# Two table changes of the activation engine put on even slots, with the C product behind the slot's second scan

## The chip, the cores and the metric

The kernel runs on one core of one Trainium2 chip. The metric is device time in microseconds (us). The core's engines run side by side, each working through its own queue in order: PE multiplies matrices into PSUM, DVE works elementwise and does the scans, ACT evaluates functions, POOL does elementwise work on SBUF, and SP issues most of the DMAs.

## The reference, cut to what matters

Two layers are applied to an input of 4 images, 512 channels and 64x64 positions. The first is a state-space layer (Mamba), run on the 512 channels in four chunks of 128, the second a linear attention. The change touches the first layer. Cut down, for one chunk of one image:

```python
xi, z = jnp.split(jnp.einsum('bld,ed->ble', x, in_proj_w), 2, axis=-1)
xc  = silu(causal_conv4(xi) + conv_b)                  # 256 inner channels
dbc = jnp.einsum('bld,ed->ble', xc, x_proj_w)          # dt (8 columns), B (16), C (16)
dt  = softplus(einsum(dbc[..., :8], dt_proj_w) + dt_proj_b)
# for every token t, 256 channels x 16 states:
h = exp(dt_t[:, :, None] * A) * h + (dt_t * x_t)[:, :, None] * B_t[:, None, :]
y = jnp.einsum('bds,bs->bd', h, C_t)
# then
out = einsum((y + xc * D) * silu(z), out_proj_w) + skip * x
```

A layer norm stands ahead of the chunks and another behind them, followed by a 512x512 projection that is added to the input. The attention layer then needs statistics of the whole image before it can start.

## The kernel before, in words

**Steps and slots.** The tokens of an image (4096) are cut into 8 tiles of 512 (`T`). A step `n` is one chunk `c` (0 to 3) of one tile of one image: 4 images x 8 tiles x 4 chunks = 128 steps (line 1006). A step has 16 slots `s` (`SLOTS`, line 674). The 256 channels x 16 states of a step are laid out as 32 blocks of 128 partitions x 512 tokens: two channel halves `e`, four groups of states `q` and four blocks `j`. A slot handles two blocks, so two slots (an even one with `jj == 0`, an odd one with `jj == 1`) share one h tile of four blocks. There are two h tiles in turn (line 733).

**A slot** (`slot`, line 725). POOL builds the input of the slot two ahead, `bx = d * B` (`drive`, line 721). DVE does two scans (line 739); each reads a decay `dA` from PSUM, which ACT has made with an exponential (`decay`, line 713) three scans ahead (`LEAD`, three PSUM buffers: the decay for scan k+3 is issued behind scan k, whose buffer it takes). In the even slot, after its first scan, DVE multiplies the previous pair's h tile by C (`product`, line 759), for 384 of the 512 columns; POOL does the other 128 in the odd slot before (line 751). Then `fold_states` (line 761) has PE make the next C in PSUM (`c_row`, one buffer, so it waits for the product), and sum h over the states into `y` by eight matmul records (the fold); where a channel half begins (the products in slots 2 and 10), the D term's diagonal matmuls go ahead of the fold. The next pair but one may write its h tile only when the fold is done.

**What else a slot carries** (`after`, line 1108, called at the slot's end). Everything else of the step is dealt out by hand over the slots, and stands in each engine's queue behind the slot's scans:

| slot | before the change |
|---|---|
| 1 | half 1 of the step's dt and dt*x is spread over partitions (SP, line 639); gate of the previous step (POOL, line 781) |
| 2 | `time_banks`: matmuls of dt for the next step into two PSUM banks `pt` (PE) |
| 3 | softplus table loaded, `time_steps` (two softplus, line 620), exponential table loaded again (ACT) |
| 3, 5, 6, 7 | four half convolutions of step n+2 (`front`, four matmul records each, PE); 8, 9: the z half |
| 4 | `to_rows`: `dt*x` (POOL, line 628), whose two writes `d_rows` to DRAM follow one slot later (SP, line 631); `out_proj` of the previous step (PE, 12 records) |
| 6 | `with_skip` copies out_proj's result (ACT, line 792) |
| 9 | gate of the current step; half 0 of the next step is spread |
| 10 | silu of step n+2 between two table loads (ACT, line 1048) |
| 12 to 15 | x projection of step n+2 |

**Filler.** The layer norms and projections (`ahead`, `late`) and the attention of the previous image (`rest`) are generators that are asked for one piece at a time, at the end of a slot (lines 1161 to 1171). They share three PSUM banks `ps_w` with the rest: a piece that needs a bank must find fewer than `limit` held, which is 1 in slots 1 to 5 and 2 otherwise. PE's time is planned by a credit: each slot adds 3.5 matmul units (one unit is an fp32 matmul of 512 columns) less what the slot's own work took, capped at 2.6; a piece of the queues `late` and `rest` begins only while the credit is positive, and one that has begun (`"more"`) is finished in the next slot. Vector operations over a whole tile (2.26 us) are marked `"wide"` and wait for a slot in `AWAY`, in which ACT is away for its table change.

`AWAY` therefore names the slots of the two table changes. The lines that decide are these:

```python
    AWAY = (3, 10)
...
            if i == 0 and jj == 0 and g:
                product(g - 1)
                fold_states(g - 1, last)
...
                    limit[0] = 1 if 0 < s < 6 else 2
                    credit = min(credit + 3.5 - (work["mm"] - seen), 2.6)
```

Of the kernel before, what the change touches and what calls it, by code (L numbers as in the profile page):

```python
# [24 lines left out]
def kernel(  # L25
# [90 lines left out]
    limit, norming = [0], []  # L116
# [258 lines left out]
    def bc(v, n):  # L375
        return v.unsqueeze(1).to_broadcast([P, n, v.shape[-1]])
# [295 lines left out]

    JJ = NJ // 2
    SLOTS = NH * NQ * JJ
    AWAY = (3, 10)

    def place(g):

        n, r = divmod(g, SLOTS)
        e, r = divmod(r, NQ * JJ)  # L680
        return n, e, *divmod(r, JJ)
# [10 lines left out]
    def b_row(g):  # L692
        n, e, q, _ = place(g)
        b_all[g // JJ] = wk.tile([P, T], F32, tag="b_all", name=f"b_all_{g}", bufs=3)
        for_states(b_all[g // JJ], fs[n]["b_rows"], q)

    def c_tail(g):
        n, e, q, _ = place(g)
        c_sb[g // JJ] = wk.tile([P, T - CUT], F32, tag="c_sb", name=f"c_sb_{g}", bufs=2)
        for_states(c_sb[g // JJ], fs[n]["c_rows"], q)  # L700
# [7 lines left out]
    def decay(k):  # L708

        n, e, q, jj = place(k // 2)  # L710
        j = jj * 2 + k % 2
        dAs[k] = ps_d.tile([P, T], F32, tag="dA", name=f"dA_{k}")
        nc.scalar.activation(  # L713
            dAs[k], fs[n]["d_all", e][:, 0, j, :], AF.Exp, scale=a_t[:, e, j, q : q + 1]
        )

    def drive(g):

        n, e, q, jj = place(g)
        bxs[g] = wk.tile([P, 2, T], F32, tag="bx", name=f"bx_{g}", bufs=3)  # L720
        nc.gpsimd.tensor_tensor(  # L721
            bxs[g], fs[n]["d_all", e][:, 1, jj * 2 : jj * 2 + 2, :], bc(b_all[g // JJ], 2), ALU.mult
        )

    def slot(g, last, after):
        n, e, q, jj = place(g)
        b, t, c = steps[n]
        if g + 2 < last:
            drive(g + 2)
        if jj == 0:  # L730
            if g + 3 * JJ < last:
                b_row(g + 3 * JJ)
            hs[g // JJ] = wk.tile([P, NJ, T], F32, tag="h", name=f"h_{g}", bufs=2)
        elif g + 1 < last:
            c_tail(g + 1)
        h = hs[g // JJ]
        for i in range(2):
            j = jj * 2 + i
            nc.vector.tensor_tensor_scan(  # L739
                h[:, j, :], dAs.pop(2 * g + i), bxs[g][:, i, :],  # L740
                0.0 if t == 0 else st[:, c, e, q, j : j + 1], ALU.mult, ALU.add,
            )
            if 2 * g + i + LEAD < 2 * last:
                decay(2 * g + i + LEAD)
            if i == 0 and jj == 0 and g:
                product(g - 1)
                fold_states(g - 1, last)
        del bxs[g]
        if jj == JJ - 1:
            nc.gpsimd.tensor_copy(st[:, c, e, q, :], h[:, :, T - 1])  # L750
            nc.gpsimd.tensor_tensor(  # L751
                h[:, :, CUT:], h[:, :, CUT:], bc(c_sb.pop(g // JJ), NJ), ALU.mult
            )
        after()

    def product(g):

        own = hs[g // JJ][:, :, :CUT]
        nc.vector.tensor_tensor(own, own, bc(c_all.pop(g // JJ), NJ), ALU.mult)  # L759
# [283 lines left out]
    def step_inputs(n):  # L1043
        b, t, c = steps[n]
        return inputs(fs[n], xn[b, t], c, names[n])
# [6 lines left out]
    def add_to(queue, pieces):  # L1052
        queue.append([pieces, None])
# [40 lines left out]
    with tc.manual_schedule():  # L1094
        credit, seen, mix, held[0], held_x[0] = 0.0, work["mm"], iter(()), 0, 0
        for n, (b, t, c) in enumerate(steps):
            f, nm = fs[n], names[n]
            before = fs[n - 1] if n else None
            nxt = fs[n + 1] if n + 1 < N else None
            front = step_inputs(n + 2) if n + 2 < N else iter(())  # L1100
            last_mix, mix = mix, mixers(fs[n + 2], names[n + 2]) if n + 2 < N else iter(())
            if c == 0 and (t + 1 < NT or b + 1 < B):
                add_to(ahead, tile_norm(b, t + 1) if t + 1 < NT else tile_norm(b + 1, 0))
            if c == 0 and t == 0 and b + 1 < B:
                add_to(light, input_norm(b + 1))
            assert c != 2 or not ahead
            for s in range(SLOTS):
                def after():
                    nonlocal credit, seen
                    now[0] = n * SLOTS + s  # L1110
                    for what in [w for at, w in due if at <= now[0]]:
                        what()
                    due[:] = [d for d in due if d[0] > now[0]]
                    if s == 0 and before is not None:
                        take_y(before, n - 1, 1)
                    if s == SLOTS // 2:
                        take_y(f, n, 0)
                    if s < 2:
                        next(last_mix, None)
                    if s == 1:  # L1120
                        spread(f, 1, nm)
                        if before is not None:
                            gate(before, 1)
                    if s == 2 and nxt is not None:
                        time_banks(nxt, names[n + 1])
                    if s == 3 and nxt is not None:
                        nc.scalar.preload_act_table_set("softplus")
                        time_steps(nxt, names[n + 1])
                        nc.scalar.preload_act_table_set("natural_log_exp_and_others")
                    if s == 6 and before is not None:  # L1130
                        pb_, pt_, pc_ = steps[n - 1]
                        with_skip(before, xn[pb_, pt_], pc_)
                        if pc_ == NC - 1:
                            add_to(late, leave(pb_, pt_))
                    if s in (3, 5, 6, 7, 8, 9):
                        next(front, None)
                    if s == 4 and nxt is not None:
                        to_rows(nxt, 0, names[n + 1])
                        to_rows(nxt, 1, names[n + 1])
                    if s == 4 and before is not None:  # L1140
                        pb_, pt_, pc_ = steps[n - 1]
                        out_proj(before, xn[pb_, pt_], pc_, names[n - 1])
                    if s == 9:
                        gate(f, 0)
                        if nxt is not None:
                            spread(nxt, 0, names[n + 1])
                    if s == 10 and n + 2 < N:
                        silu(n + 2)
                        nc.scalar.preload_act_table_set("natural_log_exp_and_others")
                    if s >= 12:  # L1150
                        next(mix, None)
                    may = [
                        what for k, what in ((0, "wide"), (1, "one ahead"), (2, "two ahead"))
                        if any(a - 2 * k <= s <= a - k for a in AWAY) or (k == 2 and s == SLOTS - 1)
                    ]
                    if light and light[0][1] == "wait" or s in AWAY and not any(
                        q and q[0][1] == "wide" for q in (ahead, late)
                    ):
                        one(light)

                    limit[0] = 1 if 0 < s < 6 else 2
                    credit = min(credit + 3.5 - (work["mm"] - seen), 2.6)
                    busy = False
                    for queue in (ahead, late, rest):
                        kind = queue[0][1] if queue else None
                        if queue is ahead or kind == "free" or credit > 0 or kind == "more" and not busy:
                            start = work["mm"]
                            one(queue, ANYWHERE if queue is ahead and (c, s) > (1, 4) else may)
                            credit -= work["mm"] - start
                            busy = busy or work["mm"] - start > 1  # L1170
                    seen = work["mm"]

                slot(n * SLOTS + s, N * SLOTS, after)
            fs[n - 1].clear() if n else None
        product(N * SLOTS - 1)
        fold_states(N * SLOTS - 1, N * SLOTS)
        now[0] = None
        for _, what in due:
            what()
# [60 lines left out]
```

## Time and profile before

| | |
|---|---|
| median of three runs | 7947.08 us (7937.27 to 7951.86) |
| the profiled execution | 7963.09 us |
| its span, first to last instruction | 7961.4 us |
| mean granted TensorE clock | 0.897 |
| first scan starts, last scan ends | 122.4 us, 7493.4 us |
| busy: DVE, POOL, PE, ACT | 6977.7, 6880.5, 6453.6, 5507.6 us |
| one scan, one C product (DVE) | 1264, 1726 ns |
| one bx, one tail product (POOL) | 2367, 1270 ns |
| one decay, one table load (ACT) | 687, 1283 ns |
| silu of a step; one softplus (ACT) | 1911, 684 ns |
| dt*x of a step (POOL) | 2361 ns |

In a group's line, the text ahead of the bar is line, engine, operation, what it writes and reads with shapes, and the count. Behind the bar stand busy time in us, mean time of one in ns, then the engine's idle time just before the group and what ended most of it. A line of the timeline has start and duration in us, then the instruction; `x4` says that four alike are merged, and the bracket gives the idle time before the first and what ended it. Where several semaphores were waited for, the one named is the last by the profile, and need not be the real cause.

### The profile page before, as it was taken

How to read it: one execution, taken by the hardware profiler on the slowest of the kernel's cores; microseconds unless marked ns; L12 is line 12 of the kernel's file. 1: busy time of each engine (PE TensorE's matmuls, PEld its weight loads, DVE VectorE, ACT ScalarE, POOL GpSimd, SP SyncE). 2: the span in 40 equal slices, each digit the busy share in tenths (PEclk: the TensorE clock that was granted, in tenths of full speed). 3: DMA queues.
4: the chain of work that ended last, by engine and by line, in shares of the span. 5: the costliest groups of instructions: out<-in, count | busy, mean ns of one | idle time of the engine just before them, and what ended most of it. 6: DMA issues, size and time to landing. Idle time of an engine off the chain costs nothing.

```text
span 7961.4 us, 90563 instructions
## 1 busy us (share of the span) xinstructions
PE 6453.6 (81%) x24835; PEld 2120.0 (27%) x24880; DVE 6977.7 (88%) x5766; ACT 5507.6 (69%) x8321; POOL 6880.5 (86%) x4597
## 2 busy tenths in 40 slices
PE   5676777677789888888788888898688888888599
PEld 1121212112223222322222223332122332322144
DVE  5999999999999999989999999998999999988600
ACT  4667777777777777767777777677777777777421
POOL 4999999999999899989999899898999999889600
PEclk7888888888899999998899999899899999999799
DMA  5666666666666666777766666677666666676402
GB/s 154 167 168 166 151 155 159 160 155 167 169 179 162 151 163 159 174 189 175 174 155 171 171 157 161 155 185 189 156 167 163 161 161 159 145 194 180 112 32 90
DMA packets 829184, 1265.87 MB, mean 159 GB/s; under 512 B 183912, under 2 KB 317560, under 8 KB 816384
## 3 DMA queue, kind: packets, MB, share of 16 engines
q1 hardware_dynamic: 804736, 1222.32, 61.1%
q0 software_dynamic: 16896, 33.56, 2.4%
q10 hardware_dynamic: 7040, 4.20, 0.2%
q8 instruction: 195, 3.19, 0.2%
q14 instruction: 317, 2.60, 0.1%
HBM read 1052.78 MB, written 206.57 MB: 158 GB/s over the span
## 4 chain that ended last, share of the span: by engine, by line
DVE 33%; PE 21%; ACT 15%; DMA 12%; issue 8%; SPq 6%; POOL 6%; POOLq 0%; ACTq 0%; DVEq 0%
DVE h L739 22%; DVE h L759 9%; DMA d_all<-d_rows 7%; ACT dA L713 5%; PE pq L124 5%; POOL bx L721 4%; PE pc L124 4%; SPq L688 3%; PE y L124 3%; PE pr L124 3%; SPq L639 2%; DMA c_sb<-c_rows 2%; ACT xz L1048 2%; PE po L124 2%; ACT L1048 1%
## 5 line engine op out<-in xcount | busy, mean ns | idle before, releaser
L721 POOL TENSOR_TENSOR bx<-d_all,b_all 128x1024 f32<-128x1024 f32 x2048 | 4824.7, 2367 | 213.3 <-DVE h L739 195.1
L739 DVE TENSOR_TENSOR_SCAN h<-dA,st,bx 128x512 f32<-128x512 f32 x3584 | 4358.9, 1264 | 358.7 <-ACT dA L713 159.0
L713 ACT ACTIVATE dA<-d_all,a_t 128x512 f32<-128x512 f32 x4096 | 2752.9, 687 | 1568.5 <-DVE h L739 1521.8
L759 DVE TENSOR_TENSOR h<-h,c_all 128x1536 f32<-128x1536 f32 x1024 | 1767.5, 1726 | 0.1
L751 POOL TENSOR_TENSOR h<-h,c_sb 128x512 f32<-128x512 f32 x1024 | 1300.2, 1270 | 190.2 <-DMA c_sb<-c_rows 95.2
L124 PE MATMUL y<-h,fold 128*32 128x512 f32 x8192 | 1271.2, 696 | 71.6 <-POOL h L751 67.4
L124 PE MATMUL c_all<-parts,sel 128*128 128x384 bf16 x1024 | 369.9, 361 | 1123.3 <-DVE h L759 1121.7
L124 PE MATMUL pc<-xn,w_cv 128*128 128x512 f32 x2048 | 1045.7, 645 | 122.8 <-DVE xn L414 62.1
L124 PE MATMUL pq<-w_qk,xa 128*128 128x512 f32 x2048 | 965.5, 604 | 7.9 <-issue 5.3
L739 DVE TENSOR_TENSOR_SCAN h<-dA,bx 128x512 f32<-128x512 f32 x512 | 591.2, 1203 | 90.0 <-ACT dA L713 65.1
L124 PEld LDWEIGHTS <-sel 128*128 128x128 bf16 x1280 | 127.1, 99 | 1762.2 <-DVE h L759 1562.5
L124 PEld LDWEIGHTS pc<-xn,w_cv 128*128 128x128 f32 x2048 | 389.5, 201 | 747.1 <-issue 424.7
L124 PEld LDWEIGHTS pq<-w_qk,xa 128*128 128x128 f32 x2048 | 398.6, 196 | 439.6 <-issue 422.4
L124 PE MATMUL pr<-xb,m 128*128 128x512 f32 x1024 | 485.3, 612 | 7.5 <-DMA xb<-x 3.6
L124 PE MATMUL pp<-xn,w_pr 128*128 128x512 f32 x1024 | 477.7, 597 | 4.8 <-DVE xn L414 4.8
L124 PEld LDWEIGHTS y<-h,fold 128*32 128x32 f32 x8192 | 170.6, 114 | 644.0 <-issue 344.9
L124 PE MATMUL y<-xz,dg 32*32 32x512 f32 x2048 | 337.3, 734 | 0.0
L781 POOL TENSOR_TENSOR xz<-xz 128x512 f32<-128x512 f32 x256 | 325.7, 1272 | 9.2 <-ACT xz L778 9.2
L832 ACT ACTIVATE kq<-pq 128x512 f32<-128x512 f32 x256 | 150.5, 588 | 259.9 <-PE pq L124 259.2
L124 PE MATMUL pd<-xz,w_xp 128*128 128x512 f32 x512 | 323.4, 764 | 7.8 <-ACT xz L1048 7.8
L628 POOL TENSOR_TENSOR dt<-dt,xz 128x1024 f32<-128x1024 f32 x128 | 302.3, 2361 | 24.7 <-ACT dt L620 24.6
L124 PE MATMUL pz<-xn,w_z 128*128 128x512 f32 x512 | 275.4, 631 | 11.7 <-ACT xz L608 8.2
(179 smaller groups left out, 6034.1 us busy)
## 6 DMA issues: line engine op xcount, KB each, us to landing
d_all<-d_rows SPq DMA_DIRECT2D x2048, 256.0 KB, 6.7
b_all<-b_rows SPq DMA_DIRECT2D x4096, 64.0 KB, 2.2
d_rows<-dt SPq DMA_DIRECT2D x256, 512.0 KB, 3.6
c_sb<-c_rows SPq DMA_DIRECT2D x4096, 16.0 KB, 1.8
xs<-in_x_dram SPq DMA_DIRECT2D x32, 1024.0 KB, 6.3
xn<-in_x_dram SPq DMA_DIRECT2D x32, 1024.0 KB, 6.2
xr<-in_x_dram POOLq DMA_DIRECT2D x32, 1024.0 KB, 10.7
x<-xr SPq DMA_DIRECT2D x32, 1024.0 KB, 4.2
```

The costliest lines, as they stand in the source:

```text
L124: nc.tensor.matmul(out_, lhsT, rhs, **how)
L628: nc.gpsimd.tensor_tensor(f["both"][:, 1], f["both"][:, 0], f["xz"][:, 0], ALU.mult)
L639: nc.sync.dma_start(d[k * BLK : (k + 1) * BLK, v], src)
L688: nc.sync.dma_start(dst[k * BLK : (k + 1) * BLK, :], rows_[q * KS + k, :].partition_broadcast(BLK))
L713: nc.scalar.activation(dAs[k], fs[n]["d_all", e][:, 0, j, :], AF.Exp, scale=a_t[:, e, j, q : q + 1])
L721: nc.gpsimd.tensor_tensor(bxs[g], fs[n]["d_all", e][:, 1, jj * 2 : jj * 2 + 2, :], bc(b_all[g // JJ], 2), ALU.mult)
L739: nc.vector.tensor_tensor_scan(h[:, j, :], dAs.pop(2 * g + i), bxs[g][:, i, :], 0.0 if t == 0 else st[:, c, e, q, j : j + 1], ALU.mult, AL ...
L751: nc.gpsimd.tensor_tensor(h[:, :, CUT:], h[:, :, CUT:], bc(c_sb.pop(g // JJ), NJ), ALU.mult)
L759: nc.vector.tensor_tensor(own, own, bc(c_all.pop(g // JJ), NJ), ALU.mult)
L781: nc.gpsimd.tensor_tensor(f["xz"][:, 1, e, :], f["xz"][:, 1, e, :], f["xz"][:, 0, e, :], ALU.mult)
L832: nc.scalar.activation(qk[i], pq, AF.Relu)
L1048: nc.scalar.activation(fs[n]["xz"], fs[n]["xz"], AF.Silu)
```

## The change

The first table change moves from slot 3 to slot 4, so that both stand on even slots, in which there is a C product. In slots 4 and 10 the product, with C and fold behind it, is issued after the slot's second scan instead of after the first. What hangs on the first table change moves one slot later too: the dt matmuls (2 to 3), the softplus (3 to 4), the first half convolution (3 to 4), `to_rows` and `out_proj` (4 to 5, and so the `d_rows` writes from 5 to 6), `with_skip` (6 to 7, and with it the start of a tile's closing norm and projection). The second to fourth half convolutions stay. The tight bank limit now holds in slots 1 to 6. No operation is added or removed.

```diff
-    AWAY = (3, 10)
+    AWAY = (4, 10)
...
-            if i == 0 and jj == 0 and g:
+            if i == int(g % SLOTS in AWAY) and jj == 0 and g:
                 product(g - 1)
                 fold_states(g - 1, last)
...
-                    if s == 2 and nxt is not None:
+                    if s == 3 and nxt is not None:
                         time_banks(nxt, names[n + 1])
-                    if s == 3 and nxt is not None:
+                    if s == 4 and nxt is not None:
                         nc.scalar.preload_act_table_set("softplus")
                         time_steps(nxt, names[n + 1])
                         nc.scalar.preload_act_table_set("natural_log_exp_and_others")
-                    if s == 6 and before is not None:
+                    if s == 7 and before is not None:
                         pb_, pt_, pc_ = steps[n - 1]
                         with_skip(before, xn[pb_, pt_], pc_)
...
-                    if s in (3, 5, 6, 7, 8, 9):
+                    if s in (4, 5, 6, 7, 8, 9):
                         next(front, None)
-                    if s == 4 and nxt is not None:
+                    if s == 5 and nxt is not None:
                         to_rows(nxt, 0, names[n + 1])
                         to_rows(nxt, 1, names[n + 1])
-                    if s == 4 and before is not None:
+                    if s == 5 and before is not None:
                         pb_, pt_, pc_ = steps[n - 1]
                         out_proj(before, xn[pb_, pt_], pc_, names[n - 1])
...
-                    limit[0] = 1 if 0 < s < 6 else 2
+                    limit[0] = 1 if 0 < s < 7 else 2
```

## The prediction, made before the result was known

> **What bounds the kernel now.** I read the page first, then the groups by form, the waits, and the timelines of single steps. A step is one 512-token tile of one channel chunk: 16 slots, 32 scans, 128 steps in all.
>
> ```profile
> span 7961.4 us, 90563 instructions
> ...
> PE 6453.6 (81%) x24835; PEld 2120.0 (27%) x24880; DVE 6977.7 (88%) x5766; ACT 5507.6 (69%) x8321; POOL 6880.5 (86%) x4597
> ...
> L721 POOL TENSOR_TENSOR bx<-d_all,b_all 128x1024 f32<-128x1024 f32 x2048 | 4824.7, 2367 | 213.3 <-DVE h L739 195.1
> L739 DVE TENSOR_TENSOR_SCAN h<-dA,st,bx 128x512 f32<-128x512 f32 x3584 | 4358.9, 1264 | 358.7 <-ACT dA L713 159.0
> ...
> L759 DVE TENSOR_TENSOR h<-h,c_all 128x1536 f32<-128x1536 f32 x1024 | 1767.5, 1726 | 0.1
> ```
>
> No engine is the bound everywhere. Scans start at 122 us and end at 7493 us, so a step takes (7493-122)/128 = 57.6 us; DVE is busy 54.0 us of it (the windows view gives 6913 us busy in that stretch) and POOL 53.6 (6866 us). I took the idle time of DVE from the timeline, scan by scan, for the 124 inner steps: about 3.1 us a step stand before scans. The places that matter: before the second scan of slot 5 0.62 us and of slot 12 0.52 (both wait for a decay, behind the table changes of slots 3 and 10), before the first scan of slot 8 0.79, of slot 12 0.37, of slots 6 and 10 0.18 and 0.20. A first scan of an even slot waits for PE (the fold that frees one of the two h tiles) or for POOL (bx).
>
> Slot 10 of one step, ACT and then DVE (start, duration, instruction):
>
> ```profile
> 2930.25 0.69 ACT L713 ACTIVATE dA<-d_all,a_t 128x512 f32<-128x512 f32 x1 [0.42 <-DVE h L739]
> ...
> 2931.47 1.28 ACT L1048 ACT_TABLE_LOAD   x1
> 2932.76 1.91 ACT L1048 ACTIVATE xz<-xz 128x2048 f32<-128x2048 f32 x1
> 2934.69 1.28 ACT L1149 ACT_TABLE_LOAD   x1
> ```
> ```profile
> 2930.44 3.70 DVE L739 TENSOR_TENSOR_SCAN h<-dA,st,bx 128x512 f32<-128x512 f32 x3
> 2934.07 1.73 DVE L759 TENSOR_TENSOR h<-h,c_all 128x1536 f32<-128x1536 f32 x1
> 2937.32 4.81 DVE L739 TENSOR_TENSOR_SCAN h<-dA,st,bx 128x512 f32<-128x512 f32 x4 [1.53 <-ACT dA L713]
> ```
>
> Three decays are ready ahead; they and one product cover 3.70+1.73 us, ACT is away longer, DVE stands 1.53 us. The same step between slots 4 and 8, PE and then DVE:
>
> ```profile
> 2904.24 3.61 PE L124 MATMUL pc<-xn,w_cv 128*128 128x512 f32 x4 [1.43 <-DVE xn L414]
> ...
> 2908.80 0.34 PE L124 MATMUL c_all<-parts,sel 128*128 128x384 bf16 x1
> 2909.06 1.06 PE L124 MATMUL y<-h,fold 128*32 128x512 f32 x8
> ...
> 2911.05 1.98 PE L124 MATMUL po<-xz,w_op 128*128 128x512 f32 x4
> ...
> 2914.80 1.88 PE L124 MATMUL pc<-xn,w_cv 128*128 128x512 f32 x4
> 2916.52 1.88 PE L124 MATMUL pq<-w_qk,xa 128*128 128x512 f32 x4
> ...
> 2918.49 1.06 PE L124 MATMUL y<-h,fold 128*32 128x512 f32 x8
> ```
> ```profile
> 2919.73 1.28 DVE L739 TENSOR_TENSOR_SCAN h<-dA,st,bx 128x512 f32<-128x512 f32 x1 [2.79 <-ACT kq L832]
> ```
>
> PE has no gap from slot 4's c_all to slot 6's fold, which ends at 2919.55; only then does slot 8's scan start. The named releaser (kq) had long been irrelevant: the fold came last. Over 124 steps slot 6's fold has a median slack of -0.13 us: PE is the bound in this stretch in over half the steps.
>
> **The Trainium skill.** "ScalarE: Activation LUTs", What ACT_TABLE_LOAD costs, gives 1283 ns a load plus a drain of some 1380 ns. The load agrees (1283 in the groups); the drain is not seen (2934.69+1.28 to 2935.99, the next ACTIVATE), so I price 1.28. "TensorE: Matmul & The Clock Gate", The HAM clock gate, says that PE falls to half clock after about 3.4 us idle; the trace agrees: after 4.76 us of idling at 2898.11 the eight y matmuls took 1.93 us instead of 1.06. "Perfetto Trace Analysis", Optimization Strategy, says that consistent bubbles can mean too few buffers; here the two h tiles are such a case.
>
> **The change, part by part.**
>
> Product behind the second scan, slots 4 and 10: adds no instruction. At slot 10 the window after the second scan grows from 3 scans + 1 product to 3 scans + 2 products: +1.73 us. ACT gains that only where it stood waiting for the second scan. Against it, fold and c_all wait one scan (1.26) longer, while slot 12's first scan keeps its time: 2.53 us after the product's end, against a chain of c_all, eight diagonal and eight fold matmuls of 2.38. Going through each step's recorded times with these three rules, slot 12 costs 0.54 instead of 0.84 us: **gain 0.31 us a step** (0.6 in the chunks c=1 and 3, 0.2 at c=2, nothing at c=0, where a 2.26 us layer-norm subtraction already covers it). Bounds: 0.1 (fold later than recorded) and 0.5 (all of the scan's wait).
>
> First table change from slot 3 to 4: before, the window was scan, product, scan, scan; now product, three scans, product: also +1.73. The 0.62 us are 1.30 at c=0 and 1.08 at c=3; subtracting 1.73 from each step's wait leaves 0.25 and 0.20. At c=1 and 2 the layer-norm multiply (2.26) sits in slot 3 and moves along to slot 4: no wait before, none after. So up to (1.05+0.88)/4 = 0.48 us, but only if slot 8's scan can follow.
>
> PE, slots 2 to 6. In units of one 512-column fp32 matmul (about 0.93 us: two records, four in 1.88), main work goes from 3.19, 2, 4.19, 2 (slots 2 to 5) to 2.19, 1, 3.19, 5. The time banks and the first half of the convolution leave the side before slot 4's fold; half the convolution now lies behind it, with out_proj. From slot 4's product end to slot 6's fold that is 0.34+1.06+1.8+1.8+2.9+0.34+1.06 = 9.3 us, before 7.5; the DVE side has six scans and a product, 9.3, plus 2.26 at c=1 and 2. At c=1 and 2 the new conv half also waits for the multiply's PSUM bank (about 0.75; the [1.43 <-DVE xn L414] above, moved), c=1 adds mu_sums (1.0). Before, PE used the time before the product; now it idles there up to 3.5 us, limited to one work bank, its credit capped at 2.6. So any filler piece (two matmuls, 1.85 us) in slots 4 and 5 ends in DVE's wait. By the credit rule (+3.5 a slot) credit is positive at slot 4 in nearly every step, and a begun item finishes in slot 5. Costs against the recorded slot 8: c=1 0.4 without attention work (10 of 29) and 1.2 with it (19), mean 0.9; c=2 0.7 with two projection pieces (now one), 1.2 with attention, mean 0.9; c=3 0.2 (0.5 gained where no filler runs, up to 2.6 lost where an item begins in slot 4).
>
> dt multiply (2361 ns, L628), slot 4 to 5 on POOL: it now stands behind bx of slot 5, the state copy and the tail product. Where POOL is continuous the sum is unchanged and the fold even gets its tail earlier. Where the tail waits for c_sb, it was the dt multiply that was done beforehand:
>
> ```profile
> 2614.51 1.27 POOL L751 TENSOR_TENSOR h<-h,c_sb 128x512 f32<-128x512 f32 x1 [1.78 <-DMA c_sb<-c_rows]
> 2615.74 4.68 POOL L721 TENSOR_TENSOR bx<-d_all,b_all 128x1024 f32<-128x1024 f32 x2
> ...
> 2618.14 1.28 DVE L739 TENSOR_TENSOR_SCAN h<-dA,st,bx 128x512 f32<-128x512 f32 x1 [1.77 <-POOL bx L721]
> ```
>
> There bx for slot 8 comes up to 2.36 us later. This is c=0 with attention running, 17 of 28 steps: 1.6 each (between 0.5 and 2.4), less 0.4 gained in the others: mean 0.8.
>
> First half: (0.8+0.9+0.9+0.2)/4 = **0.70 us lost**, the 0.48 already inside; bounds -0.4 (filler displaced) and +1.2.
>
> At nothing: d_rows' two DMAs, slot 5 to 6, pass slot 6's four b_all issues on SP (0.43 each); they are read in slot 9, some 10 us later, landing in 3.6; without that cover 1.8 us. with_skip still follows out_proj by two slots, though PE ends out_proj later; ACT then waits up to 1 us with decays queued behind it, under three ready decays. limit 1 in slot 6: filler ran there little, its credit near or under zero. Relief: with PE's credit negative after slot 5 less filler runs in slots 6 to 9; slot 10's 0.20 halves: -0.1. Attention of the third image ended two steps before the scans did; pieces left over would lengthen the tail (0 to 20 us; I take 0).
>
> **Sum.** +0.70-0.31-0.10 = +0.29 us a step, times 128 = +37 us. Against the profiled execution's 7963.1 (span 7961.4, 1.7 around it) 8000; that execution is 16 above the median of the runs, so 7947+37 = **7984**.
>
> **Rivals.** Cover wins, PE keeps up (faster): filler yields as its credit is spent and the tail's earlier place on POOL frees the fold; then slot 8 costs no more and 0.31 plus half of 0.48 stay: 0.55x128 = 70 us, **7877**. For: DVE leads the chain of waits (33%), and both decay waits sit exactly behind the table loads. Against: slot 6's fold is late already. It decides the sign once PE's extra lateness at slot 6 is under about 0.6 us. Cancelling: **7947**, if that lateness is 0.6. Worse: slot 12's fold too meets a cold PE (0.9 us more in chain, 2.38 against 2.53): another 0.5 us a step, **8048**. That the product is skipped can't be: 4 and 10 are both even, so jj is 0.
>
> **Chances.** Slower as summed 0.56, worse 0.10, cancelling 0.14, faster 0.20. About 0.2% (16 us) is what this measurement can tell from no change. Range 7890 to 8060: under it part of the faster rival, above it the worst of the bounds.
>
> **What would show it.** Right: the waits for dA in slots 5 and 12 nearly gone, slot 8's first-scan wait up from 0.8 to about 1.5 us and longer after PE's fold, or bx at c=0; PE idle before slot 4's c_all up. Wrong: slot 8's wait not grown, or dA waits that stay.

## The result, and the profile after

| | before | after |
|---|---|---|
| median of six runs each, taken together | 7948.88 us | 8159.65 us (8149.52 to 8170.71) |
| the profiled execution (its span) | 7963.09 (7961.4) us | 8159.4 (8157.5) us |
| last scan ends | 7493.4 us | 7684.9 us |
| a step (first to last scan / 128) | 57.59 us | 59.08 us |
| mean granted TensorE clock | 0.897 | 0.883 |

The change makes the kernel slower by 211 us; the ratio after to before is 1.0268, interval 1.0254 to 1.0281. Of the 196 us between the two spans 191 lie in the 128 steps (1.49 us each), the first scan starts 0.8 later, and the rest behind the last scan is 4.6 longer.

The page of the kernel after: span, busy times, chain of waits by engine, then the groups. Behind it, the chain and the fold's group of the kernel before.

```profile
span 8157.5 us, 90726 instructions
...
PE 6577.6 (81%) x24880; PEld 2134.9 (26%) x24880; DVE 6975.3 (86%) x5766; ACT 5515.7 (68%) x8321; POOL 6886.1 (84%) x4597
...
PE 32%; DVE 30%; ACT 11%; DMA 10%; issue 7%; SPq 5%; POOL 5%; DVEq 0%; POOLq 0%; ACTq 0%
...
L721 POOL TENSOR_TENSOR bx<-d_all,b_all 128x1024 f32<-128x1024 f32 x2048 | 4819.3, 2368 | 244.8 <-DVE h L739 222.6
L739 DVE TENSOR_TENSOR_SCAN h<-dA,st,bx 128x512 f32<-128x512 f32 x3584 | 4351.2, 1264 | 512.7 <-PE y L124 226.6
...
L124 PE MATMUL y<-h,fold 128*32 128x512 f32 x8192 | 1329.8, 726 | 40.0 <-POOL h L751 36.5
```
```profile
DVE 33%; PE 21%; ACT 15%; DMA 12%; issue 8%; SPq 6%; POOL 6%; POOLq 0%; ACTq 0%; DVEq 0%
...
L124 PE MATMUL y<-h,fold 128*32 128x512 f32 x8192 | 1271.2, 696 | 71.6 <-POOL h L751 67.4
```

DVE, ACT and POOL do what they did before, to 0.2%. Two things changed: DVE idles 154 us longer before the scans of this group (358.7 to 512.7), and what ends most of that is now a fold (y) where it was a decay; and the same fold matmuls take 726 ns where they took 696, 59 of the 124 us that PE is busy longer. PE leads the chain with 32% (before 21%, with DVE at 33%).

The same step as before the change (a chunk c=1), between slots 4 and 8, PE and then DVE:

```profile
2999.64 1.41 PE L124 MATMUL pt<-dt,w_dt 32*128 32x512 f32 x4
3004.92 0.50 PE L124 MATMUL c_all<-parts,sel 128*128 128x384 bf16 x1 [3.88 <-DVE h L759]
3005.35 1.94 PE L124 MATMUL y<-h,fold 128*32 128x512 f32 x8
3007.22 3.78 PE L124 MATMUL pc<-xn,w_cv 128*128 128x512 f32 x4
...
3012.05 1.99 PE L124 MATMUL pc<-xn,w_cv 128*128 128x512 f32 x4
...
3018.97 1.07 PE L124 MATMUL y<-h,fold 128*32 128x512 f32 x8
```
```profile
3014.82 1.28 DVE L739 TENSOR_TENSOR_SCAN h<-dA,st,bx 128x512 f32<-128x512 f32 x1 [0.19 <-ACT dA L713]
3020.20 1.28 DVE L739 TENSOR_TENSOR_SCAN h<-dA,st,bx 128x512 f32<-128x512 f32 x1 [4.10 <-PE y L124]
```

PE stands 3.88 us for slot 4's product, and then runs at half speed: the fold takes 1.94 us (1.06 in this step before) and the moved conv half 3.78, while the next half, four records of the same shape, takes 1.99. Slot 6's fold ends at 3020.0, and slot 8's scan stands 4.10 us (2.79 before). The windows view shows the clock over 6 us from slot 4's c_all, in the last column but two (before, from 2908.80 on, 1.00):

```profile
3005.00:3011.00 6.00, 6.00 (x17) 1.47 (x21) 6.00 (x5) 4.18 (x6) 4.50 (x5) 0.50 0.21 67
```

DVE's idle time before scans, in us a step over the 124 inner steps:

| scan | before | after |
|---|---|---|
| slot 4, first | 0.15 | 0.44 |
| slot 5, second (decay) | 0.62 | 0.00 |
| slot 6, first and second | 0.18 | 0.21 |
| slot 8, first | 0.79 | 2.77 |
| of it: fold last, bx last | 0.50, 0.29 | 2.05, 0.72 |
| slots 7, 9, 10, 13 | 0.33 | 0.22 |
| slot 12, first and second | 0.37, 0.52 | 0.41, 0.30 |
| all scans, the others included | 3.14 | 4.56 |

The sum grows by 1.42 of the step's 1.49. Both decay waits shrank as the change meant them to. One wait, slot 8's, took back 1.98.

On PE, from slot 4's c_all to the end of slot 6's fold, the mean went from 9.35 to 12.79 us (+3.44). Each record is counted from the end of the one before it. The conv half that moved in adds 2.75, where a half at full clock takes about 1.8; the fold, the same records but slower, adds 0.58 (1.00 to 1.58); c_all 0.10, the other half 0.06, filler 0.17 (1.35 to 1.52), statistics 0.11; gaps and the rest take 0.31 off. Ahead of slot 4's c_all PE idles 2.36 us from slot 2's c_all on, 0.90 before (c=1: 3.21, c=2: 3.34); the 5.5 us that experiment 5 names for these chunks count the pause ahead of slot 2's c_all too.

The moved half was slow before the change as well: 2.43 us in the mean, and 3.61 in the step that the prediction shows. But there it ran ahead of slot 4's product, where nothing waited for it, and when c_all came PE was at full clock again.

### The profile page after: what moved, and what is told of

Its sections match the earlier page's. It is cut to its first block, busy times and chain, and to the rows that moved or that the text cites. A ratio compares the mean times of both kernels' runs of the same rounds, so it can differ in the third digit from the quotient of the medians.

```text
span 8157.5 us, 90726 instructions
## 1 busy us (share of the span) xinstructions
PE 6577.6 (81%) x24880; PEld 2134.9 (26%) x24880; DVE 6975.3 (86%) x5766; ACT 5515.7 (68%) x8321; POOL 6886.1 (84%) x4597
## 4 chain that ended last, share of the span: by engine, by line
PE 32%; DVE 30%; ACT 11%; DMA 10%; issue 7%; SPq 5%; POOL 5%; DVEq 0%; POOLq 0%; ACTq 0%
DVE h L739 18%; DVE h L759 10%; PE y L124 8%; PE pc L124 7%; DMA d_all<-d_rows 5%; PE pq L124 5%; ACT dA L713 4%; POOL bx L721 3%; PE po L124 3%; SPq L688 3%; PE pr L124 2%; PE pp L124 2%; DMA b_all<-b_rows 2%; SPq L639 2%; PE c_all L124 1%
## 5 line engine op out<-in xcount | busy, mean ns | idle before, releaser
L739 DVE TENSOR_TENSOR_SCAN h<-dA,st,bx 128x512 f32<-128x512 f32 x3584 | 4351.2, 1264 | 512.7 <-PE y L124 226.6
L124 PE MATMUL y<-h,fold 128*32 128x512 f32 x8192 | 1329.8, 726 | 40.0 <-POOL h L751 36.5
L124 PE MATMUL pc<-xn,w_cv 128*128 128x512 f32 x2048 | 1087.6, 667 | 17.1 <-ACT dt L620 6.6
L124 PEld LDWEIGHTS pc<-xn,w_cv 128*128 128x128 f32 x2048 | 407.7, 212 | 733.6 <-issue 441.7
L750 POOL COPY st<-h 128x4 f32<-128x4 f32 x1024 | 209.0, 204 | 189.2 <-DVE h L739 168.3
L592 ACT ACTIVATE xz<-pc,cb 128x512 f32<-128x512 f32 x256 | 174.0, 680 | 217.7 <-PE po L124 192.9
L124 PE MATMUL pd<-xz,w_xp 128*128 128x512 f32 x512 | 305.6, 727 | 7.8 <-ACT xz L1048 7.8
```

Source lines behind the costliest of these rows:

```text
L124: nc.tensor.matmul(out_, lhsT, rhs, **how)
L592: nc.scalar.activation(xz[:, 0, e, :], pc[e], AF.Identity, bias=cb[:, e : e + 1])
L739: nc.vector.tensor_tensor_scan(h[:, j, :], dAs.pop(2 * g + i), bxs[g][:, i, :], 0.0 if t == 0 else st[:, c, e, q, j : j + 1], ALU.mult, AL ...
```

## The experiments

Two theories stood against each other. **Amount**: PE has too much work in the stretch between slot 4's product and slot 6's fold. **Clock**: the same work is slower, since PE idles longer before it and comes to it cold, that is at a granted clock near half. The rivals put the loss elsewhere: the product's place at slot 4, or POOL's order. Times are medians; ratios stand against the kernel before, with a 95% interval. "After" and "before" name the kernel that is edited.

**1. Slot 10's part alone, on before.**

```diff
-            if i == 0 and jj == 0 and g:
+            if i == int(g % SLOTS == 10) and jj == 0 and g:
```

> The kernel before with one part of the change: the C product of slot 10 behind the second scan, nothing else. My theory (the prediction's second part): the wait for a decay in slot 12 falls from 0.52 us a step to about 0.2, the fold wait in slot 12 stays near 0.35, 0.31 us a step in all, so about 40 us faster than before (7910). Rival (the later fold eats the gain): the fold wait in slot 12 grows by 0.3 us or more and the time is that of before or above it.

7943.4 us, ratio 0.9989 (0.9983 to 0.9996): 9 us faster, not 40. Slot 12's decay wait fell from 0.52 to 0.19, but its first scan rose from 0.37 to 0.51, and slot 10 from 0.20 to 0.24. The later fold and c_all take half back, which the sum had at less.

**2. One moved part alone: the first conv half from slot 3 to 4, on before.**

```diff
-                    if s in (3, 5, 6, 7, 8, 9):
+                    if s in (4, 5, 6, 7, 8, 9):
```

> The kernel before with only the first half convolution moved from slot 3 to slot 4. My theory (PE is late for slot 6's fold because half the convolution now lies behind slot 4's product, and PE, idle before it, comes to it with a cold clock): the wait of slot 8's first scan grows from 0.8 us to about 2, 100 to 190 us slower than before. Rival (the product's later place, or POOL's dt multiply, makes the loss): within 30 us of before.

8108.15 us, ratio 1.0195 (1.0181 to 1.0209): +156 us, with no table change moved. Same chunk and step, PE:

```profile
2951.82 0.50 PE L124 MATMUL c_all<-parts,sel 128*128 128x384 bf16 x1 [0.98 <-DVE h L759]
2952.25 1.93 PE L124 MATMUL y<-h,fold 128*32 128x512 f32 x8
2954.11 2.88 PE L124 MATMUL pc<-xn,w_cv 128*128 128x512 f32 x4
```

The mean stretch grew from 9.35 to 11.74 us, and the fold is cold here too: 1.46 us in the mean, 1.00 before. The moved half does both at once: it fills PE behind the product and empties it before. Slot 8's wait grew to 1.48, not to about 2. So of the 156 us some 88 (0.69 a step) are this wait; the rest are mainly decay waits that the whole change does not have (slot 12's 0.52 to 1.05, slot 7's 0.07 to 0.29). The half alone makes about a third of the 1.98 us that slot 8 loses in the whole change. In the step shown c_all is cold though PE paused only 0.98 us just ahead of it: another pause, of 2.06 us, stands 1.86 us earlier.

**3. Filler taken out of slots 4 and 5, on after** (it runs in other slots instead).

```diff
-                    for queue in (ahead, late, rest):
+                    for queue in (ahead,) if s in (4, 5) else (ahead, late, rest):
```

> The changed kernel without pieces of projection or attention in slots 4 and 5. In the changed kernel such pieces take 1.2 us (chunk 0), 1.2, 2.5 and 1.1 us of PE between slot 4's and slot 6's c_all. My theory: slot 8's wait falls by about 1.2 us a step, 120 to 150 us faster than the changed kernel, less up to 40 us if attention of the third image runs past the scans. If POOL's bx is what slot 8 waits for: less than 40 us faster.

8057.02 us, ratio 1.0131 (1.0117 to 1.0145): 103 us faster than after, a little less than expected. The stretch fell to 11.17 us, slot 8's wait from 2.77 to 1.91. So what PE has to do in the stretch counts. This filler is a remedy more than a cause, though: all but 0.17 us of it stood there before the change.

**4. The clock, with narrow matmuls, on after:** the dt matmuls are repeated three times at the end of slot 3 (12 more records into the same banks; what they add is overwritten with the same values).

```diff
+                    if s == 3 and nxt is not None:
+                        for _ in range(3):
+                            for e in range(NH):
+                                r = slice(e * LANE, (e + 1) * LANE)
+                                nc.tensor.matmul(
+                                    nxt["pt"][e], w_dt[r, :], nxt["dtr"][r, :], start=True, stop=True
+                                )
```

> The changed kernel with work added: the dt matmuls of slot 3 are issued four times instead of once (the same result into the same banks), behind slot 3's filler, which gives PE some 3.4 us more to do per step just where it idles. If the cold clock is a main term of the loss (eight fold matmuls 1.06 to 1.8 us, the first conv half 1.75 to 2.9), it falls back by up to 1.5 us a step and the kernel is 100 to 190 us faster than the changed one (about 7970 to 8060) although PE does more. If the loss is only the amount of work behind the product, or POOL's, the time is that of the changed kernel or up to 100 us more.

8211.58 us, ratio 1.0322 (1.0306 to 1.0338): 52 us slower than after. The clock from 4 to 10 us behind slot 3's last scan rose from 0.78, 0.58, 0.64, 0.85 (c=0 to 3) to 0.93, 0.67, 0.79, 0.97; the fold fell from 1.58 to 1.25 us and the first conv half from 2.75 to 2.46. But c_all itself started 1.07 us later in the mean (1.34 and 1.65 at c=0 and 3, whose pause of 1.66 and 1.24 us is too short for the added work). One effect covers the other, so this run does not tell the theories apart.

**5. The clock again, with full matmuls, on after:** in chunks 1 and 2 only, four fp32 matmuls of 128x128 by 512 columns go into the two pt banks ahead of the dt matmuls, which overwrite them.

```diff
+                        if c in (1, 2):
+                            for k in range(4):
+                                nc.tensor.matmul(
+                                    nxt["pt"][k % 2], w_z[:, 0:P], w_pr[:, k, :],
+                                    start=True, stop=True,
+                                )
```

> The changed kernel with four full 128x128 fp32 matmuls of 512 columns (about 3.7 us) put ahead of the dt matmuls in slot 3 of chunks 1 and 2, into the two banks that the dt matmuls then start afresh. They lie in PE's idle stretch before slot 4's product (5.5 us in these chunks). If the clock is half of the loss there, slot 4's fold returns from 1.8 to 1.1 us and the first conv half from 3.1 to 1.8, slot 8 waits about 2 us less in half of the steps: 100 to 130 us faster than the changed kernel (about 8040). If the clock only follows the narrow fold matmuls, or what counts is the amount of work behind the product: 40 us or less either way.

8074.89 us, ratio 1.016 (1.0144 to 1.0175): 85 us faster than after, with 3.7 us more of PE work in half the steps. The same step, PE, and the clock in the 6 us from slot 4's c_all:

```profile
2960.39 3.70 PE L1128 MATMUL pt<-w_pr,w_z 128*128 128x512 f32 x8
2964.02 1.13 PE L124 MATMUL pt<-dt,w_dt 32*128 32x512 f32 x4
2965.67 0.34 PE L124 MATMUL c_all<-parts,sel 128*128 128x384 bf16 x1 [0.53 <-DVE h L759]
2965.94 1.06 PE L124 MATMUL y<-h,fold 128*32 128x512 f32 x8
2966.93 1.98 PE L124 MATMUL pc<-xn,w_cv 128*128 128x512 f32 x4
```
```profile
2965.60:2971.60 6.00, 5.93 (x25) 1.76 (x25) 6.00 (x6) 5.02 (x8) 4.51 (x4) 1.00 0.55 125
```

Clock 1.00 in place of 0.50, fold 1.06 in place of 1.94, conv half 1.98 in place of 3.78. Over all steps of c=1 and 2 the fold went from 1.80 and 1.79 us to 1.00 in both, the first conv half from 3.20 and 2.96 to 1.91 and 1.92; at c=0 and 3, left alone, both stayed to within 0.07. Nothing was taken out of the stretch (filler is 1.52 us, as in after), so this gain is the clock's. It is a little under the forecast of 100 to 130.

**6. Clock and filler together** (5 and 3).

> The changed kernel with both remedies that helped alone: the four full matmuls ahead of slot 3's dt matmuls in chunks 1 and 2 (85 us faster than the changed kernel), and no pieces of projection or attention in slots 4 and 5 (103 us faster). If the two are separate terms of PE's lateness at slot 6's fold, most of both adds up: 150 to 190 us faster than the changed kernel, about 7985. If either alone already takes PE out of the bound, or POOL's bx becomes it: 110 us or less.

7960.5 us, ratio 1.0011 (1.0002 to 1.002): 199 us faster than after, against 85+103 = 188. A step takes 57.60 us as before the change, slot 6's fold costs slot 8 0.50 us as before. So the two remedies add up and give back the whole loss. They do not undo its causes one by one: the moved conv half still stands in the stretch (10.05 us, 9.35 before), and the filler's leaving makes up for it. What is left of slot 8's wait is bx: 0.92, where it was 0.29 before.

**7. The product at slot 4 behind the first scan again, on after.**

```diff
-            if i == int(g % SLOTS in AWAY) and jj == 0 and g:
+            if i == int(g % SLOTS == 10) and jj == 0 and g:
```

> The changed kernel with slot 4's product back behind the first scan (slot 10's stays behind the second). My theory: slot 4's fold and all of PE behind it start 1.26 us earlier and warmer, slot 8's wait falls by 1.3 to 2 us a step, the decay wait comes back by about 0.5 us (now before slot 6's or 7's scan), 100 to 190 us faster than the changed kernel. Rival (the moved convolution and out_proj alone make the loss, the product's place does nothing): within 40 us of the changed kernel.

8218.14 us, ratio 1.0326 (1.031 to 1.0341): 58 us slower than after, where 100 to 190 faster was expected. So it is not the product's place that makes PE late. The same step:

```profile
3015.25 0.34 PE L124 MATMUL c_all<-parts,sel 128*128 128x384 bf16 x1 [2.70 <-DVE h L759]
3015.52 1.78 PE L124 MATMUL y<-h,fold 128*32 128x512 f32 x8
3018.62 3.78 PE L124 MATMUL pc<-xn,w_cv 128*128 128x512 f32 x4 [1.32 <-DVE xn L414]
```

c_all and fold come a scan earlier, but the conv half behind them doesn't: here it waits for a PSUM bank that DVE's layer-norm multiply (L414) or the softplus must read empty first, and it starts as late as in after (6.6 us behind slot 3's end in the mean, 6.7 in after), and cold. In turn the decay cover is lost (slot 6's second scan 0.14 to 0.50, slot 7 0.04 to 0.23).

**8. dt\*x on POOL back in slot 4, on after.**

```diff
-                    if s == 5 and nxt is not None:
+                    if s == 4 and nxt is not None:
                         to_rows(nxt, 0, names[n + 1])
```

> The changed kernel with the dt multiply and the d_rows writes back in slot 4, so that on POOL the multiply stands ahead of slot 5's bx and tail again. If PE's fold is the main cause: only the share of slot 8's wait that is put down to bx goes (0.3 to 0.4 us a step), 30 to 60 us faster than the changed kernel. If POOL's order is the main cause: 150 us or more faster.

8155.22 us, ratio 1.0249 (1.0232 to 1.0266): as after, where 30 to 60 us were expected. The bx share of slot 8's wait fell from 0.72 to 0.15, and the fold's rose from 2.05 to 2.35. bx was late beside the later fold.

**9. Slot 10's part taken out of after.**

```diff
-            if i == int(g % SLOTS in AWAY) and jj == 0 and g:
+            if i == int(g % SLOTS == 4) and jj == 0 and g:
```

> The changed kernel with slot 10's product back behind the first scan. If slot 10's part gains 0.31 us a step: about 40 us slower than the changed kernel (8200), with the decay wait in slot 12 up by 0.3 us. If that part does nothing or harms: the same or faster.

8211.71 us, ratio 1.0319 (1.0304 to 1.0335): 52 us slower than after, as expected. Slot 12's decay wait is 0.85 without it, 0.30 with it. It is worth more here than alone (9 us), because the wait that it removes is larger here than in before (0.52). Why ACT comes later to slot 12 in this kernel was not tried.

**10. The conv half moved past slot 6's fold** (slot 5's piece to slot 6), on after, and on before with slot 10's part (there with 3 in place of 4).

```diff
-                    if s in (4, 5, 6, 7, 8, 9):
+                    for _ in range({4: 1, 6: 2, 7: 1, 8: 1, 9: 1}.get(s, 0)):
                         next(front, None)
```

> The changed kernel with the second half convolution moved from slot 5 to slot 6 (two halves in slot 6), so that only one half lies between slot 4's and slot 6's product, as before the change. If the amount of work ahead of slot 6's fold makes the loss: that stretch of PE shortens by 1.85 us, slot 8's wait falls from 2.8 to about 1.2 us, 150 to 200 us faster than the changed kernel (about 7980). If the cold clock alone makes it: 40 us or less. If PE is late throughout slots 4 to 10: the wait moves to slot 10's first scan.

> The kernel before with slot 10's product behind the second scan and with the second half convolution in slot 6. By the same theory slot 8's wait, of which 0.5 us a step is the fold's, loses 0.3 to 0.5 us and slot 10's part another 0.1 to 0.2: 50 to 80 us faster than before (about 7890). If slot 8 falls back on POOL's bx at once: 10 to 30 us faster.

On after 8135.1 us, ratio 1.0231 (1.0215 to 1.0246): only 25 us faster. Slot 8's wait falls by 1.07 (its fold share by 1.41, while bx's rises by 0.34), but slot 9 rises from 0.04 to 0.53 and slot 10 from 0.12 to 0.60. On before 7958.35 us, ratio 1.0005 (0.9999 to 1.0012), no gain either: slot 8 at 0.43, slot 10 at 0.76. PE is late through slots 4 to 10: slot 10's first scan waits for the next fold (0.52 of its wait), and slot 9's second for a decay (why ACT is late there was not tried).

**11. Slot 10's part with no filler in slots 4 and 5, on before** (1 and 3).

> The kernel before with slot 10's product behind the second scan (9 us faster than before) and no pieces of projection or attention in slots 4 and 5, where they take 1.4 us of PE a step. If the fold share of slot 8's wait (0.5 us a step) is theirs: 30 to 50 us faster than before. If the pieces only push the wait into later slots, as the late convolution did: within 15 us of before.

7961.19 us, ratio 1.001 (1.0002 to 1.0018): within 15 us of before, as the second expectation has it, and 18 us slower than slot 10's part alone. Slot 8 falls to 0.18, slot 5's decay wait rises to 0.92 and slot 10 to 0.86. In before, the filler stands where it does no harm; only behind the moved work does it cost 103 us.

## Why the prediction was right in sign and wrong in size

**The mechanism stood.** PE is late with slot 6's fold, and slot 8's first scan pays. What was to show it did: slot 5's decay wait is gone, PE idles longer ahead of slot 4's c_all, slot 8's wait grew. (By the sum that wait was to become 0.79+0.48+0.70 = 1.97, though the last part said about 1.5; it is 2.77.)

**The step that failed** is "PE, slots 2 to 6", its sum of 9.3 us with every matmul at full clock, and with it the first half's 0.70 us lost. Measured, slots 4 to 8 lose 1.65 us net (-0.62 at slot 5, +0.29, +0.03 and -0.03 at slots 4, 6 and 7, +1.98 at slot 8). The missing 0.95 us is 122 of the 176 us by which the forecast was short. It took c_all, fold and two conv halves at 0.34+1.06+1.8+1.8 us; measured in the changed kernel they take 0.43+1.58+2.75+1.78, 1.5 us more. The prediction had seen that PE "now idles there up to 3.5 us", and had read from the trace that eight matmuls after a pause of 4.76 us take 1.93 us instead of 1.06; it used that in a rival for slot 12 and not here. Its own lines also showed the half that was to move at 3.61 us, and it priced 1.8. The Trainium skill, "TensorE: Matmul & The Clock Gate", HAM oscillation — how this bites in real kernels, describes such a case: a pause of more than about 3.4 us between bursts of matmuls, and each burst starts cold. The trace agrees (3.88 us idle, clock 0.50). Here shorter pauses do it too: in the changed kernel, of 79 pauses of 2 to 3 us just ahead of a c_all, 54 were followed by a fold of more than 1.5 us; of 141 of 3 to 4 us it was 117, of 566 under 1.5 us only 10. Experiment 5 prices the clock for half of the steps: 85 us. An error the other way hid part of it: the 0.75 us that the moved half was to wait for a PSUM bank at c=1 and 2 did not come; it follows the fold without a gap.

**Amount.** Main work was counted right: one conv half more. Filler in slots 4 and 5 was foreseen as ending in DVE's wait. Its price inside the change is 103 us or 0.8 us a step (experiment 3), while without the moved work its removal gains nothing (experiment 11). The per-chunk costs (0.9, 0.9, 0.2 for c=1 to 3) let c=3 escape, for want of any cold term: its fold and first conv half take 1.31 and 2.26 us in the stretch, about 1.00 and 1.75 at full clock, and slot 8's wait there went from 0.21 to 2.15.

**POOL's dt multiply**, 0.8 us at c=0. The bx share of slot 8 did grow (0.29 to 0.72), but experiment 8 takes it away and gains nothing. A cost beside a later one was counted as a cost. It comes back once PE is in time: bx is what slot 8 still waits for in experiment 6.

**First table change**, 0.48 foreseen: 0.62 gained. Left out was the scan behind it: slot 4's first scan +0.29 and slot 6's second +0.14.

**Slot 10's part**, 0.31 foreseen: 0.18 net in the table, 9 us alone and 52 inside the change. The step shown before has it in small. DVE, then ACT (both of after):

```profile
3029.08 1.73 DVE L759 TENSOR_TENSOR h<-h,c_all 128x1536 f32<-128x1536 f32 x1
...
3037.66 1.28 DVE L739 TENSOR_TENSOR_SCAN h<-dA,st,bx 128x512 f32<-128x512 f32 x1 [1.31 <-ACT dA L713]
```
```profile
3031.21 1.28 ACT L1048 ACT_TABLE_LOAD   x1
3032.50 1.91 ACT L1048 ACTIVATE xz<-xz 128x2048 f32<-128x2048 f32 x1
3034.42 1.28 ACT L1149 ACT_TABLE_LOAD   x1
3035.72 1.33 ACT L473 ACTIVATE sq_b<-xn,about 128x512 f32<-128x512 f32 x2
3036.96 1.28 ACT L713 ACTIVATE dA<-d_all,a_t 128x512 f32<-128x512 f32 x2
```

The product stands behind slot 10's second scan, and the decay wait is still 1.31 us (1.53 before): ACT starts its first load 2.1 us after that scan ended, and two squares of a layer norm stand ahead of the first decay. The 1.73 us of cover go into ACT's other work. That this is so in most steps was not counted.

**Relief** of 0.10 in slots 9 and 10: 0.04. **Tail** of 0: 4.6 us. **Nothing** for with_skip: its own wait isn't among the large ones, but another read of PSUM on ACT is, the conv's (L592). From the view of waits:

```profile
ACT xz L592 <- PE po L124: 192.9, 103, 5.5
```

The columns are total in us, times and longest. In before this instruction waited 32.8 us, for the conv's own matmuls (pc). Decays are queued behind it. The conv that it reads stands just ahead of out_proj in PE's queue, so it is one more sign of PE's lateness; no run here separates what it costs beside the fold.

**The rivals.** Faster and cancelling needed slot 6's fold to be under 0.6 us later; from slot 3's last scan it is 2.18 later (15.26 to 17.44). The worse one, a cold PE, was the right effect at the wrong slot: slot 12's first scan lost 0.04.

**Open:** how clock and amount divide at c=0 and 3, where the full matmuls of experiment 5 were not tried; which of the other moved parts (dt matmuls, out_proj, the bank limit) brings slot 8's wait from experiment 2's 1.48 to 2.77, since none of these was run apart; more PSUM banks for the conv half, not tried; slot 10's 9 against 52 us. No kernel beat the one before clearly: slot 10's part alone does by 0.11%.

## What to carry to other kernels

Moving a block of matmuls has two prices: the work that it adds where it lands, and the pause that it leaves behind, after which the next matmuls can run at half clock. A block that runs cold in a place where nothing waits for it, as the conv half did, brings PE up to speed for those behind it. Count PE's idle time ahead of every moved block, and take the cold durations from the trace; in this kernel a pause of 2 us was often enough. A wait that is taken from one scan must be followed to the next place where the same engine is late, before it is booked as a gain.

## What the runs showed that was not expected

Added work made the kernel faster: four unused full-size matmuls in half the steps took 85 us off 8160. The added work has to fit into the pause: in experiment 4, which added some 3 us in all four chunks, c_all came 1.07 us later in the mean and the kernel lost 52 us, though the clock rose. Experiment 5 added 3.7 us only where the pause was over 3 us, and c_all came 0.3 to 0.5 us later there. The two also differ in the shape of the matmuls (32 rows and 128), and whether the shape matters for the clock was not tried apart from this.
